# Placing one-hots ahead of the digits' transposes, and counting pairs a turn later, in the prelude of a four-layer graph network

## The chip, the cores and the metric

One core of a Trainium2 chip runs one launch of the program. The metric is device microseconds (us) of that launch, as a median over runs.

The engines are called PE (TensorE matmul), PEld (TensorE weight load), DVE (VectorE), ACT (ScalarE), POOL (GpSimd) and SP (SyncE). Each engine has its own queue of instructions and takes them in order.

## The reference, cut to what matters

The graph has 6250 nodes with 64 features and 206250 directed edges, sorted by destination. Four blocks follow one another, each with a layer norm and a relu ahead of it and a residual behind it:

```python
h = relu(layernorm(x)); x = x + sgconv(relu(sgconv(h, W3, b3)), W4, b4)   # D^-1/2 (A+I) D^-1/2
h = relu(layernorm(x)); x = x + segment_sum(norm * h[col], row)
h = relu(layernorm(x)); x = x + sqrt(mean over incoming edges of clip(gate(edge) * Vp[src] + shift(edge))**2)
h = relu(layernorm(x)); x = x + (h + P h + P P h + P P P h) / 4            # P normalised by degrees
```

The normalisations need the degree of each node. The kernel gets the degrees, and the dense adjacency matrix A with small counts in fp8, from the sorted list of edges.

## The kernel before, in words

**What is built first.** `first_stage` builds A and runs the first graph convolution beside it. The node pairs (two destinations per list) are dealt in `GC` = 25 columns of 128 lists, called c = 0 to 24. A's columns are built in 14 strips. A strip consists of 16 or 12 portions, 196 portions in all. One portion costs: `one_hots` on DVE (two comparisons, tiles `hd` and `lo`, L889), and in `placed` 16 matmuls of `lo` and `hd` into `p_a` on PE (L904) and two evictions into `strip` on ACT (L908). `opool` holds two pairs of one-hots and `p_a` has two buffers.

**The prelude's loop** (L946, 32 turns numbered i = 0 to 31) fetches and turns the lists, one column per step, in a software pipeline. In turn i it issues, in the order of the code:

- POOL: the gather `near` of column i (L949), used by DVE two turns later
- DVE: a count over `near` of column i-2 (L955, L958), which gives `exact_i`, the start of the list
- POOL: the gather `run` of column i-3 (L962), used by ACT two turns later
- ACT: `key` of column i-6 (L967), read from `p_dig`
- ACT: the two halves of `digits` of column i-5 (L974, L976), and PE's two transposes of them into `p_dig` (L979; one buffer)
- PE and ACT: `place()`, which places what stands in `waiting`: the portion whose one-hots the turn before has made
- DVE and PE, in the turns of c = i-6 = 8, 17 and 24: the counting. Three times `less` on DVE (L988: which keys of these nine or seven columns lie below a bound) and nine or seven matmuls each into `p_node` on PE (L992), then one copy into `below` on DVE (L995)
- DVE: work from the list `fill` (scans, parts of the layer norm) until it is empty, then the one-hots of one new portion (`whole`)

How much of the last step a turn takes is set by `credit`, 2.0 a turn; a portion costs 2.0. Portions made in the loop are counted in `singles`.

**Behind the loop** `below` gives the degrees (L1008; L1011 on PE; L1019 on DVE), these give `norm0` (L684 on DVE, the square root L685 on ACT, L686 on DVE), and `norm0` scales the features (L1118) that are split into the three bf16 parts of U (L1119 to L1125). Then the remaining portions are made two at a time (`one_hots(..., 2)`), if need be after one more single portion so that an even number is left. Between portions PE runs the convolution's matmuls, `p_sum` (L1045, 2401 in all), 12 to 19 behind each portion; L1040 starts each sum.

**The order of instructions** on PE, DVE, ACT and POOL is the order of the code: the whole of `first_stage` stands in a `manual_schedule` of these four engines. The later stages (the gathers over A with `p_acc`, L1195; the edges' block with `Vp_dram`; the last three propagations) are not touched.

Of the kernel before, what the change touches and what calls it, by code (L numbers as in the profile page):

```python
# [8 lines left out]
F32 = mybir.dt.float32  # L9
BF16 = mybir.dt.bfloat16  # L10
# [3 lines left out]
OP = mybir.AluOpType  # L14
AX = mybir.AxisListType

P = 128
N = 6250
D = 64
NB = 49  # L20
# [569 lines left out]
GC = -(-NG // P)  # L590
# [27 lines left out]
def fast(ctx, tc, bad, x, src, dst, edge_attr, W3, b3, W4, b4, w1, b1, w2, b2, Bw, Bb, Cw, Cb,  # L618
         pAw, pAb, pBw, pBb, out):

    nc = tc.nc
# [137 lines left out]
    def first_stage(ph):  # L759

        ipool = ph.enter_context(tc.tile_pool(name="ipool", bufs=1, reuse_waits="tile"))
        rpool = ph.enter_context(tc.tile_pool(name="rpool", bufs=3, reuse_waits="tile"))
        spool = ph.enter_context(tc.tile_pool(name="spool", bufs=3, side="right", reuse_waits="tile"))
        psum = ph.enter_context(tc.tile_pool(name="ps0", bufs=1, space=PSUM, reuse_waits="tile"))
# [7 lines left out]
        with tc.tile_pool(name="dpool", bufs=1, reuse_waits="tile") as dpool:  # L772
# [11 lines left out]
                op0=OP.mult)  # L784
# [12 lines left out]
                                           op0=OP.mult, op1=OP.add)  # L797
# [26 lines left out]
        count = ipool.tile([P, 128, GQ], BF16, name="count")  # L824
# [10 lines left out]
        key = ipool.tile([P, 2, GC * P], BF16, name="key")  # L835
        below = ipool.tile([P, 3, GC], F32, name="below")
# [38 lines left out]
        def portions(s):  # L875

            lo, hi = OF_CHUNK[s % 2]
            return (hi - lo) * P // 2 // (2 * SG)
# [17 lines left out]
        def placed(s, q, n, lo, hd):  # L896

            if q == 0:
                strips[s] = new_strip()
            for r in range(2 * n):  # L900
                p = psum.tile([P, SG, P], F32, name="p_a", bufs=2)
                for j in range(SG):
                    g = r * SG + j
                    nc.tensor.matmul(p[:, j, :2 * NB], lo[:, g // GQ, :, g % GQ],  # L904
                                     hd[:, g // GQ, :, g % GQ], start=True, stop=True)
                col = 2 * (q * 2 + r) * SG

                nc.scalar.activation(  # L908
                    strips[s][:, :, col:col + 2 * SG].rearrange("p b (j l) -> p b j l", l=2),
                    p[:, :, :2 * NB].rearrange("p j (b l) -> p b j l", l=2), AF.Copy,  # L910
                    saturate=False)
                if r % 2:
                    if q + n == portions(s) and r == 2 * n - 1:
                        lo_, hi_ = OF_CHUNK[s % 2]
                        (nc.sync if s < CS - 1 else nc.scalar).dma_start(
                            strip_of(s, slice(0, NB)).bitcast(BF16),
                            strips[s][:, :, :(hi_ - lo_) * P].bitcast(BF16))
                    yield
# [3 lines left out]
        def place():  # L922
            while waiting:
                for _ in placed(*waiting.pop(0)):
                    pass
# [17 lines left out]

        near_of, run_of, digits_of, credit, singles = {}, {}, {}, 0.0, 0
        jobs = [(s, q) for s in range(CS) for q in range(portions(s))]
        for i in range(GC + 7):  # L946
            if i < GC:
                near_of[i] = rpool.tile([P, LOOK, 2], F32, name="near2")
                nc.gpsimd.indirect_dma_start(  # L949
                    out=near_of[i].rearrange("p e t -> p (e t)"), out_offset=None, in_=pairs[:, :],  # L950
                    in_offset=bass.IndirectOffsetOnAxis(ap=begin_i[:, i:i + 1], axis=0))
            if 0 <= i - 2 < GC:
                c = i - 2
                n = rpool.tile([P, 1], F32, name="n")
                nc.vector.tensor_scalar(junk[:, :LOOK], near_of.pop(c)[:, :, 0],  # L955
                                        start_of[:, c:c + 1], 0.0,
                                        op0=OP.is_lt, op1=OP.add, accum_out=n)
                nc.vector.tensor_add(exact_i[:, c:c + 1], begin[:, c:c + 1], n)  # L958
            if 0 <= i - 3 < GC:
                c = i - 3  # L960
                run_of[c] = rpool.tile([P, P, 2], F32, name="run")
                nc.gpsimd.indirect_dma_start(  # L962
                    out=run_of[c].rearrange("p e t -> p (e t)"), out_offset=None, in_=pairs[:, :],
                    in_offset=bass.IndirectOffsetOnAxis(ap=exact_i[:, c:c + 1], axis=0))
            if 0 <= i - 6 < GC:
                c = i - 6
                nc.scalar.activation(key[:, :, c * P:(c + 1) * P],  # L967
                                     digits_of.pop(c)[:, :2 * P].rearrange("p (k s) -> p k s", k=2),
                                     AF.Copy)
            if 0 <= i - 5 < GC:  # L970
                c = i - 5
                run = run_of.pop(c)
                digits = rpool.tile([P, 2, P], BF16, name="digits")
                nc.scalar.activation(digits[:, 0, :], run[:, :, 0], AF.Identity,  # L974
                                     bias=minus[:, c:c + 1])
                nc.scalar.activation(digits[:, 1, :], run[:, :, 1], AF.Copy)  # L976
                p = digits_of[c] = psum.tile([P, 1024], BF16, name="p_dig")
                for k in range(2):
                    nc.tensor.transpose(p[:, k * P:(k + 1) * P], digits[:, k, :], ident_b)  # L979
            place()  # L980
            if 0 <= i - 6 < GC:
                c = i - 6
                if c % 9 == 8 or c == GC - 1:
                    c0 = c // 9 * 9
                    p = psum.tile([P, 512], F32, name="p_node")
                    for k in range(3):
                        less = rpool.tile([P, 9 * P], BF16, name="less", bufs=2)
                        nc.vector.tensor_scalar(  # L988
                            less[:, :(c + 1 - c0) * P], key[:, 0, c0 * P:(c + 1) * P],
                            float(k * NB), None, op0=OP.is_lt)  # L990
                        for i_ in range(c0, c + 1):
                            nc.tensor.matmul(p[:, k * 9 + i_ - c0:k * 9 + i_ - c0 + 1],  # L992
                                             less[:, (i_ - c0) * P:(i_ - c0 + 1) * P],
                                             count[:, 1, 0:1], start=True, stop=True)
                    nc.vector.tensor_copy(  # L995
                        below[:, :, c0:c + 1],
                        p[:, :27].rearrange("p (k i) -> p k i", k=3)[:, :, :c + 1 - c0])
            credit += 2.0
            while credit > 0:
                cost, f, *args = fill.pop(0) if fill else (2.0, whole, *jobs[singles])  # L1000
                singles += f is whole
                f(*args)
                credit -= cost
        assert singles <= portions(0) + portions(1) and not fill

        for h in range(2):
# [2 lines left out]
        p = psum.tile([P, 512], F32, name="p_node")  # L1009
# [124 lines left out]
        p = psum.tile([P, SG, P], F32, name="p_a", bufs=2)  # L1134
        nc.tensor.transpose(p[:, 0, :], W3_sb, ident)
        nc.vector.tensor_copy(W3T, p[:, 0, :])
        p = psum.tile([P, SG, P], F32, name="p_a", bufs=2)
# [35 lines left out]
    with ExitStack() as ph, tc.manual_schedule(  # L1173
            engines={ET.PE, ET.DVE, ET.Activation, ET.Pool}):
        norm0, norm3, V3, b4_r, hidden = first_stage(ph)
# [195 lines left out]
    with ExitStack() as ph:  # L1371
        cpool, w1_d, w2_d, b1_c, b2_c, BC, bias, src_g, lane, own, count = made.pop()
# [330 lines left out]
    with ExitStack() as ph:  # L1703
        apool = ph.enter_context(tc.tile_pool(name="apool", bufs=6, reuse_waits="tile"))
        wpool = ph.enter_context(tc.tile_pool(name="wpool", bufs=2, reuse_waits="tile"))
        psum = ph.enter_context(tc.tile_pool(name="ps4", bufs=1, space=PSUM, reuse_waits="tile"))
# [90 lines left out]
```

## Time and profile before

| what | value |
|---|---|
| time, median of 3 runs | 3458.58 us (3456.76 to 3461.30) |
| profiled execution | 3455.87 us, its span 3454.10 us |
| busy over the span | PE 2697.9 us (78%), DVE 2449.7 us (71%), ACT 1228.7 us (36%), POOL 1602.8 us (46%) |
| mean granted TensorE clock | 0.929 |
| PE busy, 64 to 88 us (in the prelude's loop) | 13.15 of 24 us; DVE 20.13, ACT 16.18, POOL 15.96 |
| PE busy, 220 to 260 us (portions in pairs) | 37.68 of 40 us; DVE 39.97, ACT 29.91, POOL 0.00 |

Times in the timeline are microseconds from the start of the span. A row gives start, duration, engine, line, operation, output and input tiles, how many instructions were merged, and in brackets the idle time before it with what ended that. The prelude's loop lies between about 25 and 121 us; portions are placed in it from 55.69 us on; the sums of the first convolution start at 129.19 us, the pairs of portions at 137.47 us, and the first stage's last sums end at 523.8 us.

### The profile page before, as it was taken

How to read it: one execution, taken by the hardware profiler on the slowest of the kernel's cores; microseconds unless marked ns; L12 is line 12 of the kernel's file. 1: busy time of each engine (PE TensorE's matmuls, PEld its weight loads, DVE VectorE, ACT ScalarE, POOL GpSimd, SP SyncE). 2: the span in 40 equal slices, each digit the busy share in tenths (PEclk: the TensorE clock that was granted, in tenths of full speed). 3: DMA queues.
4: the chain of work that ended last, by engine and by line, in shares of the span. 5: the costliest groups of instructions: out<-in, count | busy, mean ns of one | idle time of the engine just before them, and what ended most of it. 6: DMA issues, size and time to landing. Idle time of an engine off the chain costs nothing. (4 is left out here: it accounts for less than half of the span.)

```text
span 3454.1 us, 58599 instructions
## 1 busy us (share of the span) xinstructions
PE 2697.9 (78%) x23087; PEld 2111.3 (61%) x23087; DVE 2449.7 (71%) x4786; ACT 1228.7 (36%) x2073; POOL 1602.8 (46%) x1885
## 2 busy tenths in 40 slices
PE   2799999999966666776776777677677678799999
PEld 1688889999944444443443444344344344499999
DVE  7899993532268869978986997997799697731111
ACT  4677770000034333443344344444334344310000
POOL 5000001000057777777777777777777777500000
PEclk9999999999978888898898898899899989999999
DMA  4234347565443322332332333232233223346664
GB/s 129 77 86 102 78 129 250 189 203 188 130 136 88 91 54 69 90 83 72 97 82 79 88 95 82 76 95 82 67 89 94 82 67 87 87 160 203 200 210 144
DMA packets 255434, 389.54 MB, mean 113 GB/s; under 512 B 96409, under 2 KB 169289, under 8 KB 254894
## 3 DMA queue, kind: packets, MB, share of 16 engines
q1 hardware_dynamic: 190542, 320.69, 29.8%
q0 software_dynamic: 54816, 60.71, 7.5%
q10 hardware_dynamic: 9792, 4.31, 0.6%
q8 instruction: 184, 3.01, 0.3%
q14 instruction: 100, 0.82, 0.1%
HBM read 341.34 MB, written 44.21 MB: 112 GB/s over the span
## 5 line engine op out<-in xcount | busy, mean ns | idle before, releaser
L1528 POOL DMA_INDIRECT v<-Vp_dram,src_g x1616 | 1534.3, 949 | 884.9 <-DMA e<-in_edge_attr 392.8
L1555 PE MATMUL p_bc<-BC,h 128*128 128x256 f32 x1616 | 510.1, 471 | 397.1 <-DVE m L1573 396.8
L1195 PE MATMUL p_acc<-U,piece 128*128 128x192 bf16 x9604 | 799.6, 246 | 2.5 <-DVE zg L1206 2.5
L1195 PEld LDWEIGHTS <-piece 128*128 128x128 fp8e4 x9604 | 794.0, 98 | 7.3 <-issue 7.0
L1555 PEld LDWEIGHTS p_bc<-BC,h 128*128 128x128 f32 x1616 | 361.8, 233 | 609.1 <-issue 511.2
L1206 DVE TENSOR_REDUCE zg<-p_acc 128x128 f32<-128x384 f32 x112 | 56.3, 507 | 494.8 <-PE p_acc L1195 494.2
L1439 DVE SCALAR_TENSOR_TENSOR junk<-p_sum,there 128x2048 bf16<-128x2048 fp8e4 (+1 forms) x112 | 361.9, 3231 | 8.7 <-PE p_sum L1434 8.5
L1581 ACT ACTIVATE m<-m 128x512 bf16<-128x512 f32 x202 | 127.2, 630 | 650.1 <-DVE m L1574 638.1
L908 ACT ACTIVATE strip<-p_a 128x784 fp8e4<-128x784 f32 x392 | 301.0, 821 | 102.3 <-PE p_a L904 95.9
L1572 DVE TENSOR_TENSOR m<-p_bc,v 128x512 f32<-128x512 f32 x202 | 139.5, 690 | 246.4 <-issue 109.6
L1587 DVE TENSOR_SCALAR to<-count,lane 128x128 bf16<-128x128 bf16 x1616 | 293.4, 274 | 0.0
L1595 PE MATMUL p_s<-m,to 128*128 128x192 bf16 x1616 | 194.9, 272 | 100.3 <-DVE H L1609 68.6
L1545 PE MATMUL p<-h,w_d 128*128 128x512 f32 x404 | 220.9, 629 | 54.4 <-ACT h L1549 54.4
L1549 ACT ACTIVATE h<-p,b_c 128x512 f32<-128x512 f32 x404 | 257.3, 695 | 3.6 <-PE p L1545 3.5
L1595 PEld LDWEIGHTS <-to 128*128 128x128 bf16 x1616 | 150.1, 108 | 172.8 <-DVE H L1609 106.9
L751 PE MATMUL p_sum<-piece,U 128*64 128x448 fp8e4 x2016 | 227.3, 364 | 30.4 <-DVE m L1660 16.1
L1562 DVE TENSOR_TENSOR p_bc<-p_bc,bias 128x1024 f32<-128x1024 f32 x202 | 247.8, 1227 | 1.2 <-PE p_bc L1555 0.7
L1567 ACT ACTIVATE p_bc<-p_bc 128x512 f32<-128x512 f32 x202 | 117.6, 582 | 344.8 <-DVE p_bc L1562 344.7
L1045 PE MATMUL p_sum<-U,strip 128*128 128x192 bf16 x2401 | 230.1, 247 | 0.0
L889 DVE TENSOR_TENSOR lo<-count,key 128x4096 bf16<-128x4096 bf16 (+1 forms) x108 | 225.9, 2091 | 0.0
L751 PEld LDWEIGHTS <-U 128*64 128x64 bf16 x2016 | 116.3, 112 | 165.3 <-issue 69.6
L1545 PE MATMUL p<-eT,w_d 128*128 128x512 f32 x404 | 216.5, 618 | 0.0
(206 smaller groups left out, 3087.1 us busy)
## 6 DMA issues: line engine op xcount, KB each, us to landing
piece<-A SPq DMA_DIRECT2D x243, 784.0 KB
e<-in_edge_attr SPq DMA_DIRECT2D x202, 256.0 KB
v<-Vp_dram,src_g POOLq DMA_INDIRECT x1616
A<-strip SPq DMA_DIRECT2D x7, 3136.0 KB
there<-A SPq DMA_DIRECT2D x196, 112.0 KB
A<-strip SPq DMA_DIRECT2D x6, 2352.0 KB
piece<-A SPq DMA_DIRECT2D x7, 448.0 KB
A<-strip ACTq DMA_DIRECT2D x1, 2352.0 KB
```

Source lines behind the costliest of these rows:

```text
L751: nc.tensor.matmul(p[half * D:(half + 1) * D, :w], U3[:, b, k, :], at_block, start=(i < 2), stop=(i >= 3 * n - 2))
L908: nc.scalar.activation(strips[s][:, :, col:col + 2 * SG].rearrange("p b (j l) -> p b j l", l=2), p[:, :, :2 * NB].rearrange("p j (b l) -> ...
L1045: nc.tensor.matmul(p[:, d * 3 * D:(d + 1) * 3 * D], strips[s][:, b, (d0 - lo + d) * P:(d0 - lo + d + 1) * P], U3[:, b, :, :].rearrange("p ...
L1195: nc.tensor.matmul(p[d // 2][:, d % 2 * 3 * D:(d % 2 + 1) * 3 * D], t[:, b, d * P:(d + 1) * P], U3[:, k * CB + b, :, :].rearrange("p t f - ...
L1439: nc.vector.scalar_tensor_tensor(junk[:m, :a1 - a0], p[:m, :a1 - a0, :].bitcast(COUNT).rearrange("p a (r j) -> p a r j", j=4), 15.5, of_th ...
L1528: ask = nc.gpsimd.indirect_dma_start(out=v[:, j, :], out_offset=None, in_=Vp_dram[:, :], in_offset=bass.IndirectOffsetOnAxis(ap=src_g[:, g ...
L1545: nc.tensor.matmul(of[g][p], w, of[g].pop(x), start=True, stop=True)
L1549: nc.scalar.activation(of[g][t], of[g].pop(p), **how)
L1555: last_of = nc.tensor.matmul(p_bc[:, 2 * q:2 * q + 2].rearrange("p j o f -> p (j o f)"), h2[:, q * P:(q + 1) * P], BC, start=True, stop=True)
L1562: nc.vector.tensor_tensor(p_bc, p_bc, bias.unsqueeze(1).to_broadcast([P, J, 2, D]), op=OP.add)
L1587: nc.vector.tensor_scalar(to[:, j, :], count, lane[:, g, j:j + 1], None, op0=OP.is_equal)
L1595: nc.tensor.matmul(p, to[:, j, :], m3[:, j].rearrange("p t f -> p (t f)"), start=(j == 0), stop=(j == J - 1))
```

## The change

`place()` moves from the middle of the turn to its top, ahead of `near`, `key`, `digits` and the transposes. The counting is cut into four steps (three comparisons with their matmuls, and the copy); the steps are queued a turn later than before (c = i-7), and one of them is issued per turn, ahead of the turn's one-hots. The loop has one turn more; steps that are left are issued behind it.

```diff
-        for i in range(GC + 7):
+        counted = []
+
+        def edges_below(c0, c):
+            p = psum.tile([P, 512], F32, name="p_node")
+
+            def one(k):
+                less = rpool.tile([P, 9 * P], BF16, name="less", bufs=2)
+                nc.vector.tensor_scalar(
+                    less[:, :(c + 1 - c0) * P], key[:, 0, c0 * P:(c + 1) * P],
+                    float(k * NB), None, op0=OP.is_lt)
+                for i_ in range(c0, c + 1):
+                    nc.tensor.matmul(p[:, k * 9 + i_ - c0:k * 9 + i_ - c0 + 1],
+                                     less[:, (i_ - c0) * P:(i_ - c0 + 1) * P],
+                                     count[:, 1, 0:1], start=True, stop=True)
+
+            def taken():
+                nc.vector.tensor_copy(
+                    below[:, :, c0:c + 1],
+                    p[:, :27].rearrange("p (k i) -> p k i", k=3)[:, :, :c + 1 - c0])
+
+            return [lambda: one(0), lambda: one(1), lambda: one(2), taken]
+
+        for i in range(GC + 8):
+            place()
             if i < GC:
                 near_of[i] = rpool.tile([P, LOOK, 2], F32, name="near2")
...
                     nc.tensor.transpose(p[:, k * P:(k + 1) * P], digits[:, k, :], ident_b)
-            place()
-            if 0 <= i - 6 < GC:
-                c = i - 6
+            if 0 <= i - 7 < GC:
+                c = i - 7
                 if c % 9 == 8 or c == GC - 1:
-                    c0 = c // 9 * 9
-                    p = psum.tile([P, 512], F32, name="p_node")
-                    for k in range(3):
-                        less = rpool.tile([P, 9 * P], BF16, name="less", bufs=2)
...
-                    nc.vector.tensor_copy(
-                        below[:, :, c0:c + 1],
-                        p[:, :27].rearrange("p (k i) -> p k i", k=3)[:, :, :c + 1 - c0])
+                    counted.extend(edges_below(c // 9 * 9, c))
+            if counted:
+                counted.pop(0)()
             credit += 2.0
...
                 credit -= cost
+        while counted:
+            counted.pop(0)()
         assert singles <= portions(0) + portions(1) and not fill
```

In the built program the order on POOL and SP is what it was. The loop makes 21 single portions and one more follows behind it (22; 20 before), and 87 pairs are left (88 before).

More of the change, by code (lines that the diff above doesn't have):

```diff
@@ L979, in first_stage @@
                     nc.tensor.transpose(p[:, k * P:(k + 1) * P], digits[:, k, :], ident_b)
-            place()
-            if 0 <= i - 6 < GC:
-                c = i - 6
+            if 0 <= i - 7 < GC:
+                c = i - 7
                 if c % 9 == 8 or c == GC - 1:
-                    c0 = c // 9 * 9
-                    p = psum.tile([P, 512], F32, name="p_node")
-                    for k in range(3):
-                        less = rpool.tile([P, 9 * P], BF16, name="less", bufs=2)
[L988 to L995, printed above, removed]
-                        below[:, :, c0:c + 1],
-                        p[:, :27].rearrange("p (k i) -> p k i", k=3)[:, :, :c + 1 - c0])
+                    counted.extend(edges_below(c // 9 * 9, c))
+            if counted:
+                counted.pop(0)()
             credit += 2.0
```

## The prediction

> **What bounds the kernel now.** I read the table of busy time by stretch first. In the prelude's loop no engine is full; once portions come in pairs DVE is.
>
> ```profile
> 64.00:88.00 24.00, 13.15 (x134) 10.97 (x135) 20.13 (x42) 16.18 (x35) 15.96 (x16) 1.00 0.26 74
> 220.00:260.00 40.00, 37.68 (x544) 34.13 (x542) 39.97 (x24) 29.91 (x40) 0.00 (x0) 1.00 0.44 108
> ```
>
> Columns: length, busy PE, PEld, DVE, ACT, POOL, clock, DMA share, GB/s. So a saving in the loop counts only if it cuts the loop's chain, and from 142 us on what counts is DVE's work. Next the timeline of one undisturbed turn:
>
> ```profile
> 79.70 0.39 ACT L967 ACTIVATE key<-p_dig 128x256 bf16<-128x256 bf16 x1
> 79.96 0.42 ACT L974 ACTIVATE digits<-run,minus 128x128 bf16<-128x128 f32 x1
> 80.26 0.33 ACT L976 ACTIVATE digits<-run 128x128 bf16<-128x128 f32 x1
> 80.44 0.49 PE L979 MATMUL p_dig<-ident_b,digits 128*128 128x128 bf16 x2 [1.55 <-ACT digits L974]
> 80.72 1.51 PE L904 MATMUL p_a<-hd,lo 128*128 128x98 bf16 x16
> 81.62 1.54 ACT L908 ACTIVATE strip<-p_a 128x784 fp8e4<-128x784 f32 x2 [1.03 <-PE p_a L904]
> 82.28 0.97 DVE L889 TENSOR_TENSOR hd<-turns,key 128x1568 bf16<-128x1568 bf16 x1 [0.80 <-PE p_a L904]
> 83.05 0.39 ACT L967 ACTIVATE key<-p_dig 128x256 bf16<-128x256 bf16 x1
> ```
>
> The turn is a ring between ACT and PE: key 0.26, digits 0.30 and 0.18 to the transposes, 0.28 to the portion's matmuls, 0.90 to the first eviction (half of the matmuls), 1.43 for the evictions: 3.35 us. DVE has slack: two one-hots take 2.04 us and the near-count 0.42, together 2.46, and it waits 0.80 for a free buffer (the bracket on `hd`). I call M(i) the placing matmuls of turn i and O(i) its one-hots; M(20) is at 80.72, M(13), the first, at 55.69. The counting breaks the ring:
>
> ```profile
> 90.16 0.83 DVE L988 TENSOR_SCALAR less<-key 128x1152 bf16<-128x1152 bf16 x2 [1.99 <-ACT key L967]
> 92.53 0.46 DVE L988 TENSOR_SCALAR less<-key 128x1152 bf16<-128x1152 bf16 x1 [1.55 <-PE p_node L992]
> 93.49 0.19 DVE L995 COPY below<-p_node 128x27 f32<-128x27 f32 x1 [0.49 <-PE p_node L992]
> 95.75 1.49 PE L904 MATMUL p_a<-hd,lo 128*128 128x98 bf16 x16 [1.44 <-DVE lo L889]
> ```
>
> Here M(23) to M(24) takes 95.75 - 90.76 = 4.99 us, 1.64 over a turn, because O(23) stands behind the counting on DVE. At the first count it is 64.03 - 59.01 = 5.02, 1.67 over. Last, the end of the loop:
>
> ```profile
> 115.18 1.23 DVE L988 TENSOR_SCALAR less<-key 128x896 bf16<-128x896 bf16 x3 [2.43 <-ACT key L967]
> 120.99 0.42 DVE L1008 TENSOR_TENSOR deg<-below 64x50 f32<-64x50 f32 x2
> 125.01 0.47 DVE L686 RECIPROCAL norm<-norm 128x49 f32<-128x49 f32 x1 [1.26 <-ACT norm L685]
> 125.51 1.16 DVE L1118 TENSOR_TENSOR z<-U,norm 128x448 f32<-128x448 f32 x2
> 155.20 1.79 DVE L889 TENSOR_TENSOR hd<-turns,key 128x3136 bf16<-128x3136 bf16 x1
> 159.10 1.79 DVE L889 TENSOR_TENSOR hd<-turns,key 128x3136 bf16<-128x3136 bf16 x1
> ```
>
> Read here when the degrees end, that `norm0` waits for its square root behind evictions on ACT, and that a pair of portions takes 3.90 us.
>
> **The change, step by step.**
>
> *Placing first.* The new order on PE is M(i), transposes(i), M(i+1); on ACT evictions(i), key, digits, evictions(i+1). M(i+1) still stands behind transposes(i), which wait for digits(i). It is the same ring, cut open elsewhere: 0 per turn. At its ends it is not 0. Digits of c=8 (turn 13) ran at 54.73 while DVE made O(12), for nothing; now they stand behind M(13), and M(14) stays at 59.01. In return the last digits (c=24) fall between M(29) and M(30), which was 114.21 - 112.44 = 1.77 and becomes 3.35: +1.58.
>
> *Gathers.* Their order on POOL is unchanged, but `run` needs the buffer that the digits read, and these come a turn later. `near` is queued behind `run`: issued at 82.17 for a reading near 91.0 it has 8.8 us; it keeps 5.5. In the table by half microseconds the bytes of the `run` issued at 99.31 move between 100.5 and 101.5: landing takes 2.2. Cost 0; without that cover, see the second rival.
>
> *The two counts inside the loop.* Each `less` (0.46) now goes ahead of one turn's one-hots. The first waits for its key, about 1.9 us as now; but the one-hots are 3.0 us ahead of their matmuls (lo ended near 77.7 for M(20) at 80.72), so M does not move. The copy waits for the third matmul group, some 3.3 us of idle DVE, and the one-hots behind it come about 0.9 us ahead of need. What is left on the ring is PE's part: nine matmuls (0.32 to 0.40 in rows alone; 0.35 taken) behind the transposes and ahead of the next M, three times. 1.05 per count in place of 1.65: from 3.31 to 2.10 together, -1.2. Bounds: 0 each (hidden) to 0.40, so -3.3 to -0.9. Replayed: M(18) at 73.45 (74.04 before), M(24) 93.5 (95.75), M(29) 111.3 (112.44), M(30) 114.65 (114.21).
>
> *The end of the loop.* Key c=24 is read by `less` at 117.4, now in turn 31, with O(31) behind it to 119.8, `less`, O(32) to 122.2, `less`, a wait of 0.6 for its matmuls, the copy, `deg` to 123.75 (121.41 before). The extra portion's one-hots (to 125.75) cover the degrees' matmuls, so the 1.25 wait of L1019 goes; the square root stands behind the evictions of O(32)'s portion on ACT until 127.4 (idle 0.8). z starts at 128.2, 2.7 later than 125.51, but with 22 portions begun in place of 20. Bounds from the waits in this chain (0 to 1.3 for the root, 0 to 0.6 for the copy): +1.5 to +3.5.
>
> *One portion's evictions inside U's split* (1.43 on ACT, at c=2). ACT idles 0.5 us per block there and gets back in step two blocks later; DVE sees 0.1. Bounds 0 and 1.0.
>
> *One pair fewer.* DVE is full from 142 to 430 us, and the matmuls behind the last hundred portions come out in the same numbers per portion, so the stage's end comes one period earlier: -3.90. If PE were the limit it would be only two portions' matmuls, 2 x 0.92 = -1.84.
>
> Sum: +2.7 + 0.1 - 3.9 = -1.1 us. Behind it PE runs on from the stage's end (97% busy from 520 to 900), so it goes through whole. The profiled execution of 3455.87 becomes 3454.8; it lies 2.7 below the median, so 3458.58 becomes 3457.5.
>
> **A rule weighed.** The row first: the loop's placing matmuls have a mean of 281 ns, 16 in 1.51 us, against 209 ns and 0.91 us in the pairs, though the clock column reads 1.00 in both. PE is busy (1.51 + 0.49) / 3.35 = 60% of a turn, and 64% with counting in it, so I keep 1.51. [...]
>
> **Rivals.**
>
> *The ring opens.* If placing no longer waited for the digits, the turn would fall to DVE's 2.46: 16 x 0.89 = 14 us, 3444. For it: ACT idles 1.03 a turn on PE. Against: the order listing has M(i+1) directly behind transposes(i).
>
> *The lists come late, slower.* With the digits a turn later, `near` has 5.5 us. It decides once landing takes more than that (2.2 seen in a quiet stretch): each us over is added to every turn from 19 to 26 or so, DVE waiting at L955 for DMA. At 6.7 us landing and 8 turns it is 8 x 1.2 = +9.6, thus 3467.1 with -1.1 counted in. For it: 16 gathers of the loop fall in 64 to 88 us. Against: DMA share is 0.26 there, and no L955 waits for DMA.
>
> *PE limits the pairs.* PE is 94% busy there (37.68 of 40). Then the pair returns 1.84 and the sum is +1.0: 3459.5. It counts as no change.
>
> **How the numbers follow.** 0.2% is 6.9 us, about what a measurement of this kernel can tell from no change. Forecast 0.58; PE-limited pairs 0.22, so same 0.80. The ring opening, or a warm PE with the low bounds, 0.11. Late lists 0.09. The bounds of the steps add up to -4.5 (counts -2.1, end -1.2, split -0.1 beside the sum) and +3.0 (+0.3, +0.8, +0.9, and +2.1 where PE limits the pairs). With the runs' own scatter of 2.7 on either side the range is 3451.4 to 3464.3.
>
> **What would show it.** Right: turns of 3.35 away from counts and 3.7 with a counting step, no DVE idle by `less` that moves a placing; `deg` near 123.3, z near 128.2, first pair near 140.3, last sums of the stage about 1 us earlier than 523.8. Wrong: turns near 2.5; L955 released by DMA; PE placing matmuls of 209 ns inside the loop; a first pair later than 142.

## The result, and the profile after

| what | before | after |
|---|---|---|
| time, median of 22 runs each | 3460.40 us (3456.76 to 3461.82) | 3464.43 us (3461.94 to 3466.24) |
| span of the profiled execution | 3454.1 us | 3461.4 us |
| last sums of the first stage end, first `p_acc` starts (us from the span's start) | 523.67 | 522.08 |
| first `zg` of the next stage (VectorE's first reduction of `p_acc`) | 554.31 | 559.47 |

The ratio is 1.0014, with a 95% interval of 1.0008 to 1.0020: 4 us slower, where 1.1 us faster was forecast. The first stage does end earlier, by 1.6 us; the stage behind it loses 6.8 us in its first 30. I show the two parts in this order.

**The first stage.** The busy time by stretch, with the columns of the prediction's first fence, is almost that of before: VectorE (DVE) is not full in the loop and full in the pairs.

```profile
64.00:88.00 24.00, 13.17 (x155) 11.02 (x153) 19.02 (x42) 16.05 (x36) 15.08 (x15) 1.00 0.25 70
220.00:260.00 40.00, 37.56 (x542) 33.91 (x541) 39.97 (x27) 29.30 (x40) 0.00 (x0) 1.00 0.47 119
```

In the timeline of after: a counting step on PE, the copy that ends a count, one undisturbed turn, the end of the loop and the first two pairs of a stretch without other work:

```profile
65.72 0.49 PE L1002 MATMUL p_dig<-ident_b,digits 128*128 128x128 bf16 x2 [1.55 <-ACT digits L997]
66.01 0.42 PE L957 MATMUL p_node<-count,less 128*128 128x1 bf16 x9
66.29 1.47 PE L904 MATMUL p_a<-hd,lo 128*128 128x98 bf16 x16
73.63 0.18 DVE L962 COPY below<-p_node 128x27 f32<-128x27 f32 x1 [2.99 <-PE p_node L957]
...
82.43 0.39 ACT L990 ACTIVATE key<-p_dig 128x256 bf16<-128x256 bf16 x1
...
83.17 0.49 PE L1002 MATMUL p_dig<-ident_b,digits 128*128 128x128 bf16 x2 [1.55 <-ACT digits L997]
83.45 1.51 PE L904 MATMUL p_a<-hd,lo 128*128 128x98 bf16 x16
84.35 1.54 ACT L908 ACTIVATE strip<-p_a 128x784 fp8e4<-128x784 f32 x2 [1.03 <-PE p_a L904]
85.78 0.39 ACT L990 ACTIVATE key<-p_dig 128x256 bf16<-128x256 bf16 x1
...
117.02 0.39 DVE L953 TENSOR_SCALAR less<-key 128x896 bf16<-128x896 bf16 x1 [2.43 <-ACT key L990]
122.71 0.42 DVE L1021 TENSOR_TENSOR deg<-below 64x50 f32<-64x50 f32 x2
126.74 0.47 DVE L686 RECIPROCAL norm<-norm 128x49 f32<-128x49 f32 x1 [0.47 <-ACT norm L685]
127.24 1.16 DVE L1131 TENSOR_TENSOR z<-U,norm 128x448 f32<-128x448 f32 x2
156.93 1.78 DVE L889 TENSOR_TENSOR hd<-turns,key 128x3136 bf16<-128x3136 bf16 x1
160.83 1.78 DVE L889 TENSOR_TENSOR hd<-turns,key 128x3136 bf16<-128x3136 bf16 x1
```

The turn is the same ring and the same 3.35 us (85.78 - 82.43). The counting matmuls stand between the transposes and the placing: placing comes 0.57 us behind the transposes' start in that turn and 0.28 in the other. No wait of `less` or of the copy moved a placing. z starts 1.73 us later than before, with two more portions in.

**The start of the next stage.** TensorE (PE) begins the gathers over A with `p_acc`, and puts the last chunk's small dense layer (`hidden`, tiles `feat`, `h`, `p_node`) between them. The timeline of before, ScalarE (ACT) and PE:

```profile
518.19 11.86 ACTq L665 DMA_DIRECT2D pAw_d<-in_L_gnn_pAw  x1
531.46 0.60 ACT L1087 ACTIVATE feat<-p_node 128x512 f32<-128x512 f32 x1 [13.93 <-issue]
532.29 1.12 PE L1092 MATMUL p_node<-feat,W3T 64*128 64x512 f32 x2
534.18 1.12 PE L1092 MATMUL p_node<-feat,W3T 64*128 64x512 f32 x2 [0.78 <-ACT h L1094]
535.24 4.22 PE L1195 MATMUL p_acc<-U,piece 128*128 128x192 bf16 x49
```

And of after:

```profile
516.62 15.95 ACTq L665 DMA_DIRECT2D pAw_d<-in_L_gnn_pAw  x1
533.96 0.60 ACT L1100 ACTIVATE feat<-p_node 128x512 f32<-128x512 f32 x1 [18.02 <-issue]
534.61 2.07 PE L1105 MATMUL p_node<-feat,W3T 64*128 64x512 f32 x2 [3.85 <-ACT feat L1100]
537.46 2.07 PE L1105 MATMUL p_node<-feat,W3T 64*128 64x512 f32 x2 [0.78 <-ACT h L1107]
539.46 5.15 PE L1208 MATMUL p_acc<-U,piece 128*128 128x192 bf16 x49
```

ACT does not idle before `feat` for want of data ("issue"): it sits in the issue of a 16 KB load, `pAw_d`, behind the strip's last write on the same queue, for 15.95 us in place of 11.86. So `feat` comes late, PE waits 3.85 us, and what follows is slower: 2.07 for 1.12 us, twice, and 5.15 for 4.22. That is 3.85 + 0.95 + 0.95 + 0.93 = 6.68 of the 6.75 us by which the way from the first `p_acc` to the first `zg` grew (30.64 to 37.39). While these matmuls run, the clock column of the table by stretch of after reads 0.51; in before it reads 1.00 from 531 to 545 us.

```profile
534.50:541.20 6.70, 5.81 (x16) 2.65 (x17) 0.00 (x0) 1.43 (x3) 5.90 (x146) 0.51 0.84 292
```

Why is the issue held longer? The pieces of A are loaded by SP's queue. The placing matmuls that end just ahead of the first load, and the row that begins with this load, before and then after:

```profile
510.66 0.90 PE L904 MATMUL p_a<-hd,lo 128*128 128x98 bf16 x16
511.60 45.91 SPq L1191 DMA_DIRECT2D piece<-A  x14
```

```profile
513.84 0.90 PE L904 MATMUL p_a<-hd,lo 128*128 128x98 bf16 x16
514.77 43.86 SPq L1204 DMA_DIRECT2D piece<-A  x13
```

The first load of a piece waits for one-hots (`lo`) to be read, and starts at 511.60 before, when the second-to-last pair has been placed, but at 514.77 after, when the last pair has. (The profile's list of waits puts SP's 15.7 and 20.6 us ahead of these loads down to DVE, which writes `lo`; in the built programs the load waits for PE alone, which reads it.) In the built program the memory of the first piece (byte 114176 on) lies over the first of `opool`'s two buffers of `lo` (113952 to 122144). The sets of one-hots take the two buffers in turn: 20 singles and 88 pairs put the last of 108 sets into the second, 22 singles and 87 pairs put the last of 109 into the first. The table by stretch shows what the early start is worth, before and then after:

```profile
511.60:517.50 5.90, 5.90 (x87) 5.73 (x85) 1.73 (x3) 4.23 (x6) 0.00 (x0) 1.00 0.84 311
517.50:530.00 12.50, 12.50 (x153) 12.49 (x152) 1.80 (x5) 0.02 (x1) 0.00 (x0) 1.00 1.01 280
```

```profile
510.00:516.00 6.00, 6.00 (x89) 5.85 (x87) 1.76 (x3) 4.30 (x6) 0.00 (x0) 1.00 0.10 16
516.00:532.50 16.50, 14.76 (x178) 14.52 (x175) 1.80 (x5) 0.00 (x0) 0.00 (x0) 1.00 1.04 326
```

Before, 5.9 us x 311 GB/s = 1.8 MB are moved ahead of the strip's write (2.4 MB, issued at 517.55); after, it is 0.1 MB, and then the DMA share reads 1.04 (516 to 532.5 us) up to the end of the held issue (532.57). The 1.7 MB left over are, as an estimate, some 5 us at 326 GB/s; the issue is held 4.09 us longer.

### The profile page after: what moved, and what is told of

Its sections match the earlier page's. It is cut to its first block, busy times and chain, and to the rows that moved or that the text cites. A ratio compares the mean times of both kernels' runs of the same rounds, so it can differ in the third digit from the quotient of the medians.

```text
span 3461.4 us, 58599 instructions
## 1 busy us (share of the span) xinstructions
PE 2695.8 (78%) x23087; PEld 2108.2 (61%) x23087; DVE 2451.4 (71%) x4788; ACT 1228.7 (35%) x2073; POOL 1605.9 (46%) x1885
## 5 line engine op out<-in xcount | busy, mean ns | idle before, releaser
L1568 PE MATMUL p_bc<-BC,h 128*128 128x256 f32 x1616 | 500.1, 464 | 392.0 <-DVE m L1586 391.6
```

Of the source, the lines that this page charges most:

```text
L1568: last_of = nc.tensor.matmul(p_bc[:, 2 * q:2 * q + 2].rearrange("p j o f -> p (j o f)"), h2[:, q * P:(q + 1) * P], BC, start=True, stop=True)
```

## The experiments

My theory: the parity of the one-hots decides when the pieces start, and through the queue of the DMAs it holds up ACT, `feat` and PE. Rivals: the new order of the first stage itself or a later stage costs the time; or the late pieces cost it directly, not by way of ACT. All comparisons have 11 or 12 runs of the kernel and 33 or 35 of the kernel before. One of them (e5, e8, e9, e10) ran on a slower chip, where the kernel before took 3979 us and scattered by 43; its times (-8.2, -3.4, -7.3 and -0.8 us against before, in this order) decide nothing, its stretches by profile do, and three of its kernels were run again.

| kernel | one-hots' last buffer | first `p_acc` | `feat` | first `zg` | `p_acc` to `zg` | time against before | ratio, 95% interval |
|---|---|---|---|---|---|---|---|
| before | 2nd | 523.67 | 531.46 | 554.31 | 30.64 | | |
| after | 1st | 522.08 | 533.96 | 559.47 | 37.39 | +4.0 | 1.0008 to 1.0020 |
| e1_after_slot | 2nd | 521.83 | 529.66 | 552.48 | 30.65 | -3.1 | 0.9980 to 0.9998 |
| e2_before_slot | 1st | 523.53 | 535.24 | 560.89 | 37.36 | +8.1 | 1.0012 to 1.0030 |
| e3_place_first | 2nd | 531.06 | 538.87 | 563.35 | 32.29 | +7.2 | 1.0012 to 1.0030 |
| e4_count_later | 1st | 517.80 | 529.51 | 555.86 | 38.06 | +0.5 | 0.9991 to 1.0009 |
| e5b_after_pool | 1st | 522.24 | 526.99 | 554.54 | 32.30 | -2.0 | 0.9984 to 1.0002 |
| e6_before_pool | 2nd | 524.30 | 529.04 | 554.94 | 30.64 | -1.6 | 0.9987 to 1.0005 |
| e8b_later_slot | 2nd | 517.90 | 525.89 | 548.57 | 30.67 | -6.4 | 0.9974 to 0.9992 |
| e9b_later_pool | 1st | 517.74 | 522.48 | 550.03 | 32.29 | -6.8 | 0.9971 to 0.9989 |

(Starts in us of one profiled execution each, time as a difference of medians in us.)

### e1_after_slot and e2_before_slot: the buffers changed round, nothing else

In both kernels, at the first pair (e1 is after with this, e2 before); in the traces the four `memset` take 0.06 us each:

```diff
+        skipped = [opool.tile([P, GB // GQ, t.shape[1], GQ], BF16, name=name)
+                   for name, t in (("lo", count), ("hd", turns))]
+        for t in skipped:
+            nc.vector.memset(t[:, 0, 0, :], 0.0)
         ready = one_hots(*jobs[0], 2)
+        for t in skipped:
+            nc.vector.memset(t[:, 0, 0, :], 0.0)
```

> The kernel after, with one tile of each kind of one-hots (lo, hd) taken and freed unused around the first pair, so that all pairs change places in the two buffers and the last pair of the first stage lies where it lay in the kernel before. Theory (which buffer the last pair lies in decides when the adjacency pieces of the next stage may be loaded): the first piece is issued when the second-to-last pair's matmuls end (about 511.5 instead of 514.8), the activation that makes feat starts by 531, the two p_node matmuls behind it wait for nothing, and the first zg of the next stage comes at 552.5 to 553.5 instead of 559.5 (before: 554.3). Time 1 to 2 us under the kernel before. Rival (the new order of the first stage itself, or a later stage, costs the time): the buffer changes nothing, zg near 559.5, time about 4 us over the kernel before.

> The kernel before, with the same unused pair of one-hot tiles around its first pair, so that its last pair lies in the other buffer; the order of the first stage is untouched. Theory of the buffer: the stage's last sums still start near 519.6, but the first piece is issued only when the last pair's matmuls end, some 3.2 us later than 511.6; feat and the p_node matmuls come late and the first zg at 559 to 561 instead of 554.3. Time 5 to 7 us over the kernel before. Rival (the order of the first stage): no difference from the kernel before, within 1 us.

Measured: -3.1 and +8.1 us, and the stretch from `p_acc` to `zg` simply changes owner: 30.65 in after's order of the first stage, 37.36 in before's. The timeline of e1:

```profile
516.36 11.91 ACTq L665 DMA_DIRECT2D pAw_d<-in_L_gnn_pAw  x1
530.45 1.12 PE L1105 MATMUL p_node<-feat,W3T 64*128 64x512 f32 x2
```

and of e2:

```profile
518.07 15.77 ACTq L665 DMA_DIRECT2D pAw_d<-in_L_gnn_pAw  x1
535.89 1.12 PE L1092 MATMUL p_node<-feat,W3T 64*128 64x512 f32 x2 [3.67 <-ACT feat L1087]
```

The theory holds, the first rival falls for this stretch: the order inside the first stage has no part in it. e1's pieces start at 509.75, where I had expected 511.5; that figure was before's and left out that e1's first stage ends earlier. Both time differences lie 1 us outside what was expected, e1 below it and e2 above it.

### e3_place_first and e4_count_later: the two halves of the change

e3 moves only `place()` to the turn's head; e4 leaves it in the middle and takes over the rest of the change (the counting a turn later, one step a turn, GC + 8 turns). e3 against before, then e4 against after:

```diff
         for i in range(GC + 7):
+            place()
...
-            place()
             if 0 <= i - 6 < GC:
```

```diff
         for i in range(GC + 8):
-            place()
...
+            place()
             if 0 <= i - 7 < GC:
```

> Half of the change: place() at the head of the turn, the counting of pairs as in the kernel before (all three steps in one turn, GC + 7 turns, 20 single portions, so 88 pairs and the last pair in the buffer it had before). By the prediction's steps the turn keeps 3.35 us, one step of 1.58 us is added where the digits of c = 24 now stand between two placings, and no pair is saved: the stage's last sums 0 to 2 us later than 519.6. Theory of the buffer: the next stage starts as in the kernel before, 17.2 us from first p_acc to the group of 392; time 0 to 2 us over the kernel before. Rival (placing first costs the time): 4 us over it.

> The other half: the counting a turn later and one step per turn (GC + 8 turns, 22 single portions, so 87 pairs and the last pair in the other buffer), place() in the middle of the turn as before. Theory of the buffer: the stage's last sums start 1 to 3 us earlier than 519.6, and the start of the next stage loses 5 to 7 us, as in the kernel after; time 3 to 5 us over the kernel before. Rival (placing first costs the time): 1 to 3 us under the kernel before.

Both were missed, inside the first stage: e3 ends it 7.4 us later than before (0 to 2 expected), e4 5.9 us earlier (1 to 3 expected). In time both lie nearer to the rival, that placing first costs it (+7.2 in e3, +0.5 in e4): it does, but inside the first stage, where its price had been taken from the prediction. In e3 the timeline shows a count:

```profile
92.78 1.51 PE L904 MATMUL p_a<-hd,lo 128*128 128x98 bf16 x16
95.53 0.83 DVE L988 TENSOR_SCALAR less<-key 128x1152 bf16<-128x1152 bf16 x2 [5.34 <-ACT key L968]
...
99.80 1.41 PE L904 MATMUL p_a<-hd,lo 128*128 128x98 bf16 x15 [2.30 <-DVE lo L889]
```

With `place()` ahead, the key that `less` needs comes behind the evictions of the portion just placed, and the next one-hots stand behind `less`: 7.02 us between two placings, 3.67 over a turn, where the kernel before lost 1.64. Placing first makes the old counting worse. In e4's timeline the counting costs nothing:

```profile
68.75 0.49 PE L1001 MATMUL p_dig<-ident_b,digits 128*128 128x128 bf16 x2 [1.33 <-ACT digits L996]
69.04 1.51 PE L904 MATMUL p_a<-hd,lo 128*128 128x98 bf16 x16
70.35 0.42 PE L957 MATMUL p_node<-count,less 128*128 128x1 bf16 x9
72.38 1.51 PE L904 MATMUL p_a<-hd,lo 128*128 128x98 bf16 x16
```

The nine matmuls fall into PE's wait for the digits (1.33 us, where an undisturbed turn has 1.55), and every turn of the loop with counting takes 3.34 us. z starts at 122.96. So of the change's two halves the counting gains and the placing loses: between e4 and after z moves by 4.28 us. Behind `p_acc` both follow their buffer: e4 loses 7.4 us more than before there, and comes out even.

### e5_after_pool, e5b_after_pool: ACT taken out of the queue

```diff
-        pAw_d = diagonal(pAw, "pAw_d", wpool)
-        pBw_d = diagonal(pBw, "pBw_d", wpool)
+        pAw_d = diagonal(pAw, "pAw_d", wpool, nc.gpsimd)
+        pBw_d = diagonal(pBw, "pBw_d", wpool, nc.gpsimd)
```

(`diagonal` issues its two loads on the engine given instead of on ACT.)

> The kernel after, with the four small loads of pAw_d and pBw_d issued by GpSimd in place of ScalarE; the last pair stays in the buffer that delays the pieces. Theory (the late pieces cost time only because ScalarE sits in the issue of pAw_d behind the strip's write and so makes feat late): feat starts near 527, p_node waits for no feat, the granted clock stays at 1.00 from 530 to 545, the first zg comes at 552.5 to 554 in place of 559.5, and the time is 1 to 3 us under the kernel before. Rival (the pieces themselves come too late, the DMA queues being full): the wait only moves from p_node to p_acc, zg stays near 558 to 560 and the time 2 to 5 us over.

> The same kernel as e5_after_pool, since the chip of that comparison was slower for every kernel (3979 us for the kernel before) and scattered by 20 us. From its trace (30.6 to 32.3 us from first p_acc to first zg, against 37.4 in the kernel after) and the stage's end of the kernel after (522.1): zg at 552.7 to 554.5, and 0 to 3 us under the kernel before. Rival (late pieces): zg near 558 to 560, 2 to 5 us over it.

The timeline of e5b:

```profile
512.40 1.14 POOL L665 DMA_DIRECT2D pAw_d<-in_L_gnn_pAw  x2 [407.32 <-DVE pBw_d L663]
526.99 0.60 ACT L1100 ACTIVATE feat<-p_node 128x512 f32<-128x512 f32 x1 [10.98 <-PE p_node L1097]
533.82 5.87 PE L1208 MATMUL p_acc<-U,piece 128*128 128x192 bf16 x49
```

The pieces are as late as in after (first issue 514.82), but `feat` waits only for PE and nobody waits for `feat`; `p_acc` to `zg` takes 32.30 in place of 37.39, and the time falls from 4 over before to 2 under it, which its interval does not tell from no difference. The late pieces cost their time by way of ACT's queue; the rival of pieces that `p_acc` waits for falls. The point I had wrong is the clock: 49 `p_acc` matmuls take 5.87 for 4.22, with a granted clock of 0.50 from 534.2 to 537.6 us, though PE had not waited for `feat` (its longest gap from the first `p_acc` on was 0.78 us, for `h`). More of that at the end.

### e6_before_pool: the same edit on before

> The kernel before, with the loads of pAw_d and pBw_d issued by GpSimd. In the kernel before ScalarE sits 11.9 us in that issue, but feat still starts at 531.46, ahead of the end of the matmuls before p_node (532.3). Theory (an idle ScalarE cost nothing there): first zg 30.6 us behind first p_acc as before, time within 1.5 us of the kernel before. Rival (ScalarE's wait costs something even there): 2 us or more under it.

Measured: 30.64 from `p_acc` to `zg`, as before; the time is 1.6 us lower (1.5 expected at most) with an interval of 0.9987 to 1.0005, so not told from no difference. ACT's 11.9 us cost before little or nothing.

### e8, e8b_later_slot and e9, e9b_later_pool: the half that gains, without the loss behind it

e4 with e1's unused tiles, and e4 with e5's edit.

> Counting a turn later and one step per turn with place() in the middle of the turn, as in e4_count_later, and the unused pair of one-hot tiles around the first pair, as in e1_after_slot, so that the last pair lies in the buffer it had before. Theory (the two effects are separate and add up): first p_acc at 517.5 to 518 as in e4_count_later, from there to the first zg 30.7 us as in before, so zg at 548.5 and 5 to 7.5 us under the kernel before. Rival (the next stage has a limit of its own, the DMA queues, so that an earlier end of the first stage is lost there): zg at 551 or later, 1 to 3 us under the kernel before.

> As e4_count_later, with the loads of pAw_d and pBw_d issued by GpSimd; the last pair in the buffer that delays the pieces. Theory: as for e5_after_pool, feat in time and no drop of the clock, so zg near 548.5 to 549.5 and 5 to 7.5 us under the kernel before, about the same as e8_later_slot. Rival (late pieces): zg near 553 to 556, 0 to 2 us under the kernel before.

> The same kernel as e8_later_slot, for the same reason. Both effects add: first p_acc at 517.5 to 518, zg at 548.5 to 550.2 (30.7 us, or 32.3 where the clock halves for one stretch of 3.4 us), 4.5 to 7.5 us under the kernel before. Rival (the gain is lost in later stages, as some 2 us seem to be between the kernel after and before): 1 to 3 us under it.

> The same kernel as e9_later_pool, for the same reason: zg at 548.5 to 550, 4.5 to 7.5 us under the kernel before. Rival (the gain is lost in later stages): 1 to 3 us under it.

Measured in e8b and e9b, on a chip where the kernel before took 3460.0 us: -6.4 and -6.8 us. These are the two fastest kernels here, faster than both before and after (by their differences from before, 10 us under after). Both effects add, and nothing of the gain is lost later; e9b's `zg` is at the end of what was expected, because its clock drops for one stretch (0.54 from 529.8 to 533.2 us; 5.87 for 49 `p_acc`) and e8b's does not (1.00; 4.22). On the slower chip it was the other way round (49 `p_acc` in 5.87 us in e8 and 4.22 in e9, `p_acc` to `zg` 32.30 and 30.65), so neither edit decides whether these matmuls are slow.

### e10_count_ahead: after, with the counting step right behind `place()`

```diff
         for i in range(GC + 8):
             place()
+            if 0 <= i - 7 < GC:
+                c = i - 7
+                if c % 9 == 8 or c == GC - 1:
+                    counted.extend(edges_below(c // 9 * 9, c))
+            if counted:
+                counted.pop(0)()
```

> The kernel after, with the counting step moved from behind the digits' transposes to directly behind place(), at the head of the turn. Theory (in the kernel after, nine counting matmuls between the transposes and the next placing lie on the ring between ScalarE and TensorE, 0.24 us in each of six turns; ahead of the transposes they fall into TensorE's wait for the digits): all turns 3.35 us, z and the stage's last sums 1.2 to 1.6 us earlier than in the kernel after (z near 125.8 of 127.24, last sums near 516.5 of 518.0); the start of the next stage keeps its loss, time 2 to 4 us over the kernel before. Rival (the counting turns are longer because VectorE's one-hots come late behind less): they stay at 3.58 us, and nothing changes.

Timeline:

```profile
99.95 1.51 PE L904 MATMUL p_a<-hd,lo 128*128 128x98 bf16 x16
101.27 0.42 PE L957 MATMUL p_node<-count,less 128*128 128x1 bf16 x9
103.01 0.49 PE L1008 MATMUL p_dig<-ident_b,digits 128*128 128x128 bf16 x2 [1.33 <-ACT digits L1003]
103.30 1.51 PE L904 MATMUL p_a<-hd,lo 128*128 128x98 bf16 x16
```

Counting turns take 3.35 us again, with `less` still ahead of DVE's one-hots: what made them longer in after was PE's part alone. From the first placing to z it is 70.10 us, against 71.25 in after: 1.15 less, just under the 1.2 expected, with 0.28 of one disturbed turn in it. The loss behind `p_acc` stays (38.68). Its time on the slower chip cannot be told from before's.

## Why the prediction was wrong

By its own steps, in the trace of after:

- **Placing first, +1.58:** the turn kept its 3.35 us and M(29) to M(30) became 3.35, as worked out. But M(14), which was to stay at 59.01, came at 59.31, and the move costs more than the one step: against e4, which has the same counting and no move, it is 4.28 at z. That is 0.29 at the first placing, 1.47 up to M(29) because the counting matmuls now lie on the ring (the prediction booked this under the counts), 1.58 there, 0.94 in the last count.
- **Gathers, 0:** right; no count over `near` waited for a DMA.
- **The two inner counts, -1.2:** 0.70 per count was left on the ring (turns of 3.63, 3.59, 3.58, then 3.30), predicted 1.05. The place on the ring was right, the size within its bounds. That M(18) came at 73.46, for 73.45 replayed, is luck: the late start and the cheaper first count cancel.
- **End of the loop, +2.7:** measured +1.73 at z (`deg` ends at 123.13, for 123.75). M(30) came at 114.27 for 114.65 replayed, the copy waited 0.44, not 0.6, and the square root cost 0.47 of idle time, not 0.8.
- **U's split, +0.1:** measured 0 (from z to the first pair 11.96 before, 11.95 after).
- **One pair fewer, -3.90:** from z to the first `p_acc` it is 398.16 before and 394.84 after, 3.32 less, between the two limits of 3.90 and 1.84; e4 has the same 394.84. What sets it between them was not tried.
- **Sum, -1.1:** -1.59 at the end of the stage. Up to here the forecast holds, by errors that partly cancel.
- **"Behind it PE runs on from the stage's end (97% busy from 520 to 900), so it goes through whole":** this step failed, and it alone turns the sign. PE's busy share says that PE was not waiting before; it does not say what keeps it from waiting. `feat` was ready 0.2 us ahead of its need (531.46 + 0.60 against 532.29). In place of -1.59 the first `zg` came at +5.16. At the last steps of the gathers (961 us) it is still +5.1. The profiled executions differ by 7.3 at their ends, the medians by 4.0: before's profiled execution lies 4.5 us under its median, after's 1.3, so the rest is taken for the scatter of single executions.

None of the rivals named this: the ring did not open, no list came late, and PE-limited pairs, priced at +1.0, act inside the first stage, which ended 1.59 earlier. The price of the pair carried its own trap. One pair fewer and two singles more change an even number of sets into an odd one, and the number of sets was in the prediction's hands; who takes the buffers' memory over was not looked up. Everything named under "what would show it" lay in the first stage, and came true or nearly so (z 127.24 for 128.2, first pair 139.19 for 140.3) while the kernel became slower.

The warm PE, which has a part in the chance of 0.11, is a term that no run shows: in the loop of after the placing matmuls kept 1.47 to 1.53 us a portion, and the clock column reads 1.00 there in before and after (64 to 88 us). A lower clock comes some 400 us later, at the loss. In after PE waits 3.85 us for `feat`, and then the clock reads 0.51 from 534.5 to 541.2 us, where it reads 1.00 in before. In e4 it falls to 0.50 2.0 us into a gap of 3.67 us and stays there for 10.2 us; in e2 it falls to 0.50 only 1.3 us after a gap of 3.67 us and stays there for 6.8 us. So in these three runs the drops do not keep to the ends of the gaps; what sets them off was not shown.

## What to carry to other kernels

A saving at the end of a stage is worth what the next stage can do with it (here its end came 1.59 us earlier, and the first `zg` 5.16 us later): look at who takes over the memory, the queues and the clock there, and how much slack that start has, before a busy share is taken as proof that a gain goes through. A change in the number of rounds through a ring of buffers moves the last round to another buffer; if the next stage's first load lies on it, the load moves by a whole round (here from 511.60 to 514.77 us). And price the parts of a change with each other, not one by one: here the placing cost 1.6 us alone on paper, 4.3 with the new counting (after against e4), and 7.4 with the old (e3 against before).

## What the runs showed of the hardware

- A load of 16 KB held the engine that issued it. The second `pAw_d` load waits for no semaphore in the built program, yet its issue takes 11.86 us in before and 15.95 us in after on ACT, behind a strided write of 2352 KB (6608 packets on that queue from 505 to 535 us, in both). The first `pAw_d` load in before, ahead of that write on the same queue, takes 0.48 us; issued by GpSimd, two such loads take 1.14 us, but they too go out ahead of the write (at 512.40 in e5b, the write at 516.03), so these runs do not part the other engine from the earlier place. What holds the issue behind the write was not measured by itself.
- In e3 the granted clock fell to 0.51 with no long idle stretch ahead: from the first `p_acc` to the drop the longest gap of PE is 0.78 us. The table by stretch (first row ahead of the drop, second the drop):

```profile
539.30:542.70 3.40, 2.62 (x11) 0.88 (x9) 0.00 (x0) 0.85 (x2) 1.59 (x17) 0.99 0.41 89
542.70:546.10 3.40, 3.40 (x23) 3.21 (x24) 0.00 (x0) 0.69 (x1) 3.40 (x106) 0.51 1.00 403
```

  PE was busy for 2.62 of 3.40 us, 2.24 of it in four float32 matmuls, and then ran 3.40 us at a clock of 0.51, 1.65 us lost (`p_acc` to `zg` 32.29 against 30.64 in before). The same sequence of instructions has its next 49 `p_acc` in 4.22 us in before, e1, e6, e8b and e9, and in 5.86 to 5.87 in e3, e5, e5b, e8 and e9b; e8 and e8b are one kernel, and so are e9 and e9b. What decides it was not shown: in e1 PE was busy for the same 2.62 of 3.40 us (529.4 to 532.8) at a clock of 1.00, and no drop came behind it.
